# The last attention's gate: sigmoid on ScalarE, or exponential on ScalarE with an addition and a reciprocal on VectorE

## The chip, the cores and the metric

The kernel runs on one core of a Trainium2 chip. A core has a matrix engine (PE; its loading of weights is listed apart as PEld), a vector engine (DVE), an engine for activation functions (ACT), a general engine (POOL), and a queue engine that only starts transfers here (SP). The engines run their own queues of instructions in order and wait for one another through semaphores. The metric is device time in microseconds, the median of several runs.

## The reference

The reference is a decoder of four layers, each with two attentions and a feed-forward part, twelve blocks in all, on an input of 8 batches x 256 positions x 128 channels. The block that the change touches is the eleventh, `L3_xattn`: 16 heads of 8 channels, causal, with a mask over keys, and a gate on the output. `query` is the normalised input, `key` and `value` are the first 256 positions of a context:

```
q, k, v = heads(query @ Wq.T), heads(key @ Wk.T), heads(value @ Wv.T)
scores = q . k / sqrt(8), masked by key and by position
context = softmax(scores) . v, heads put side by side
gate = sigmoid(query @ Wg.T + bg)
output = (gate * context) @ Wo.T
```

The gate has 8 x 256 x 128 elements, in float32.

## The kernel before, in words

Four of the twelve blocks are attentions with 16 heads, and all four are written by one function, `_heads_attention` (L469); the last of them calls it with `causal=True`, a `key_bias` and `gate=True` (L819 to L820). Its main loop (L679) goes over steps t, one head of one batch at each: t = 16 b + h, 128 steps and a tail. What belongs to a head is spread over several steps:

- At step t `maxima` (L501) makes the scores of head t on PE into a PSUM bank (`mh_sps`), and DVE finds each row's maximum, in two instructions for the causal halves (L514, into `mh_nm`). The banks are three (`ps_a`, L487), shared with the output products.
- After every fourth head, `turn` (L535) splits the four heads' maxima on POOL (three instructions, L540 to L543, into `mh_nx`). Two steps later `turned` (L545) transposes them on PE (`mh_mps`), copies them on ACT (`mh_m`, L552), and ACT starts the transfer that puts them beside the queries (L554).
- Twelve steps behind its maxima, `exps` (L556) makes the scores of the head again, transposed, lowered by the maxima and masked, on PE (`mh_bsps`), and ACT takes the exponential (`mh_e`, L574).
- Every four heads, four steps further, `combine` (L602) multiplies the exponentials with the values on PE, sixteen products for four heads (`mh_ops`), and ACT copies the result out (L617). Two of these later `divide` (L621) transposes them back (`mh_otps`), and DVE takes the reciprocals of the sums (L631, L632) and multiplies (L636, into `mh_o`). With the batch's last heads, POOL multiplies with the gate (L643). Projection, addition to x and the norm for the next block follow (L646 to L661).
- At h = 6 of each batch, ahead of that step's maxima, `gate_of` (L594) makes the batch's gate: four products on PE (`mh_gps`), the bias added on DVE (L599), the sigmoid on ACT (L600). The gate tiles, `mh_gates`, have two buffers.

Keys and queries of the next batch are projected and spread by SP's transfers during the current batch.

The order of instructions within each engine is found by a scheduler that goes by its own estimate of when the inputs are ready; among instructions that are ready the one written earlier comes first. For the products and transposes of the attentions this is switched off: they keep the order in which they are written (L451, L454). ACT computes its functions from tables, and the instruction that loads a set of tables, `ACT_TABLE_LOAD`, isn't written in the kernel: the compiler puts it in ahead of a function where needed.

Of the kernel before, what the change touches and what calls it, by code (L numbers as in the profile page):

```python
# [35 lines left out]
AF = mybir.ActivationFunctionType  # L36
ALU = mybir.AluOpType
# [307 lines left out]
class _Heads:  # L345
# [104 lines left out]
    def mm(self, *a, **kw):  # L450
        return self.E.tc.keep_in_program_order(self.E.nc.tensor.matmul(*a, **kw))  # L451
# [17 lines left out]
def _heads_attention(E, ctx, causal=False, mask=None, key_bias=None, gate=False, guest=None, known=(0,), pace=None):  # L469
# [6 lines left out]
    hd, nc, W = E.heads, E.nc, E.w(E.heads.layer)  # L476
    n, ready = hd.n, hd.ready
    nk = n // P
    scale = DH ** -0.5
# [110 lines left out]
    outs, osbs, gates = {}, {}, {}  # L590
# [3 lines left out]
    def gate_of(b):  # L594
        ps = pg.tile([P, 2, D], F32, tag="g", name="mh_gps")
        for c in range(2):
            mm(ps[:, c, :], E.xt(b)[:, c * P : c * P + P], W("wg"), start=True, stop=True)
        gates[b] = gp.tile([P, 2, D], F32, name="mh_gates")
        nc.vector.tensor_tensor(gates[b], ps, W("bg").unsqueeze(1).to_broadcast([P, 2, D]), ALU.add)  # L599
        nc.scalar.activation(gates[b], gates[b], AF.Sigmoid)  # L600

    def combine(i):  # L602

# [75 lines left out]
    while t < end or todo:  # L679
        now[0] = t  # L680
        b, h = divmod(t, H)
# [14 lines left out]
        if gate and b < B and h == 6:  # L696
            gate_of(b)
# [1058 lines left out]
```

## Time and profile before

| | us |
|---|---|
| median of 3 runs | 1811.19 (1810.04 to 1814.04) |
| the profiled execution | 1812.43 |
| its span, first to last instruction | 1810.6 |
| first and last bias addition of a gate begin (L599) | 1559.4, 1708.0 |

Busy over the whole span:

| engine | us | share |
|---|---|---|
| PE | 1485.5 | 82% |
| PEld | 1069.0 | 59% |
| DVE | 1136.2 | 63% |
| ACT | 891.7 | 49% |
| POOL | 501.6 | 28% |

Times within the trace are counted from the start of the span. A line of the timeline gives start and duration in us, the engine, the line of the kernel, the operation, the tile written and the tiles read, shape and count; in brackets stands how long the engine was idle just before, and whose work ended that idle time. The lines of waits give the engine and tile that waited, for whom, the total in us, how often, and the longest.

### The profile page before, as it was taken

How to read it: one execution, taken by the hardware profiler on the slowest of the kernel's cores; microseconds unless marked ns; L12 is line 12 of the kernel's file. 1: busy time of each engine (PE TensorE's matmuls, PEld its weight loads, DVE VectorE, ACT ScalarE, POOL GpSimd, SP SyncE). 2: the span in 40 equal slices, each digit the busy share in tenths (PEclk: the TensorE clock that was granted, in tenths of full speed). 3: DMA queues.
4: the chain of work that ended last, by engine and by line, in shares of the span. 5: the costliest groups of instructions: out<-in, count | busy, mean ns of one | idle time of the engine just before them, and what ended most of it. 6: DMA issues, size and time to landing. Idle time of an engine off the chain costs nothing. (4 is left out here: it accounts for less than half of the span.)

```text
span 1810.6 us, 29331 instructions
## 1 busy us (share of the span) xinstructions
PE 1485.5 (82%) x10141; PEld 1069.0 (59%) x10141; DVE 1136.2 (63%) x3845; ACT 891.7 (49%) x1822; POOL 501.6 (28%) x998
## 2 busy tenths in 40 slices
PE   5689999999989989777378888879837799789976
PEld 3456677766655556354256665646516677677753
DVE  4567666665636676777377777666466555455555
ACT  7245445555642345222635556456644456466631
POOL 3122222222101121333323433331113433344331
PEclk9799999999989999897689999989967899899996
DMA  4011101114000000000111111011002321111100
GB/s 151 12 36 35 26 14 37 35 32 159 9 1 1 1 1 1 0 1 1 26 43 35 36 29 34 14 36 44 11 18 54 99 54 45 51 49 49 29 1 24
DMA packets 47236, 60.43 MB, mean 33 GB/s; under 512 B 5232, under 2 KB 36976, under 8 KB 46448
## 3 DMA queue, kind: packets, MB, share of 16 engines
q1 hardware_dynamic: 44720, 56.99, 11.9%
q8 instruction: 80, 1.31, 0.3%
q10 hardware_dynamic: 2368, 1.57, 0.3%
q14 instruction: 68, 0.56, 0.1%
HBM read 14.50 MB, written 1.05 MB: 9 GB/s over the span
## 5 line engine op out<-in xcount | busy, mean ns | idle before, releaser
L451 PE MATMUL mh_sps<-mh_k,mh_q 96*128 96x512 f32 (+2 forms) x1024 | 323.5, 398 | 48.2 <-DMA mh_q<-mh_qp 23.9
L451 PE MATMUL mh_bsps<-mh_q,mh_k 128*128 128x256 f32 (+1 forms) x1536 | 354.9, 337 | 7.0 <-ACT mh_e L587 4.1
L587 ACT ACTIVATE mh_e<-mh_bsps 128x512 f32<-128x512 f32 x512 | 280.9, 600 | 119.6 <-PE mh_bsps L451 112.4
L451 PEld LDWEIGHTS mh_bsps<-mh_q,mh_k 128*128 128x128 f32 x1536 | 267.8, 199 | 32.3 <-issue 6.7
L451 PEld LDWEIGHTS mh_sps<-mh_k,mh_q 96*128 96x128 f32 x1024 | 173.3, 203 | 94.9 <-issue 46.9
L514 DVE CUSTOM_DVE_ANT_0 mh_rest<-mh_sps,mask_b 128x512 bf16<-128x512 f32 x256 | 167.1, 684 | 80.9 <-PE mh_sps L451 77.6
L451 PE MATMUL mh_ops<-mh_e,mh_v 128*32 128x256 f32 (+1 forms) x3072 | 204.9, 380 | 11.9 <-ACT mh_e L574 10.6
L533 DVE TENSOR_REDUCE mh_nm<-mh_sps 128x1 f32<-128x512 f32 x256 | 165.0, 680 | 36.9 <-PE mh_sps L451 36.4
L451 PEld LDWEIGHTS mh_ops<-mh_e,mh_v 128*32 128x32 f32 x3072 | 97.5, 113 | 85.0 <-ACT mh_e L574 21.1
L574 ACT ACTIVATE mh_e<-mh_bsps 128x384 f32<-128x384 f32 x256 | 117.2, 493 | 53.5 <-PE mh_bsps L451 30.9
L197 POOL TENSOR_SCALAR ln_rstd<-ln_mv 128x2 f32<-128x2 f32 x96 | 22.0, 229 | 404.6 <-DVE ln_mv L195 404.2
L514 DVE CUSTOM_DVE_ANT_0 mh_rest<-mh_sps,km_q 128x128 bf16<-128x128 f32 (+1 forms) x256 | 80.0, 350 | 66.2 <-PE mh_sps L451 64.5
L540 POOL CAST mh_hi<-mh_nm 128x8 fp32r<-128x8 f32 x128 | 24.8, 194 | 338.9 <-DVE mh_nm L514 203.0
L514 DVE CUSTOM_DVE_ANT_0 mh_rest<-mh_sps,causal 128x128 bf16<-128x128 f32 (+1 forms) x256 | 79.4, 352 | 54.5 <-PE mh_sps L451 51.8
L215 ACT COPY xt<-ln_ps 128x256 f32<-128x256 f32 x96 | 36.1, 376 | 128.3 <-PE ln_ps L454 65.9
L451 PE MATMUL mh_bsps<-mask_t,ident 128*128 128x512 bf16 x256 | 98.8, 386 | 0.4 <-ACT mh_e L587 0.4
L617 ACT COPY mh_osb<-mh_ops 128x256 f32<-128x256 f32 x128 | 47.6, 372 | 89.3 <-PE mh_ops L451 89.1
L552 ACT CAST mh_m<-mh_mps 8x256 fp32r<-8x256 f32 x128 | 46.1, 360 | 91.0 <-PE mh_mps L454 89.6
L882 ACT ACTIVATE moe_si<-moe_gps 128x512 f32<-128x512 f32 x64 | 38.0, 597 | 101.9 <-PE moe_gps L880 81.1
L880 PE MATMUL moe_ups<-xt,w_L_ffn 128*128 128x512 f32 x128 | 69.6, 626 | 6.9 <-ACT moe_si L882 4.8
L201 DVE TENSOR_SCALAR ln_z<-x,ln_mv,ln_rstd 128x128 f32<-128x128 f32 x128 | 41.9, 368 | 50.5 <-POOL ln_rstd L198 50.5
L891 PEld LDWEIGHTS moe_dps<-w_L_ffn,moe_act 128*128 128x128 f32 x512 | 64.1, 199 | 15.9 <-issue 7.7
(359 smaller groups left out, 3098.3 us busy)
## 6 DMA issues: line engine op xcount, KB each, us to landing
mh_k<-mh_kp SPq DMA_DIRECT2D x64, 256.0 KB
mh_q<-mh_qp SPq DMA_DIRECT2D x256, 64.0 KB
mh_k<-mh_kp SPq DMA_DIRECT2D x64, 128.0 KB
w_L_ffn<-in_w_L_ffn SPq DMA_DIRECT2D x2, 1558.0 KB
w_L_attn<-in_w_L_attn SPq DMA_DIRECT2D x2, 1056.0 KB
ctx_t<-in_ctx_t SPq DMA_DIRECT2D x4, 512.0 KB
mh_q<-mh_m ACTq DMA_DIRECT2D x128, 8.0 KB
w_L_ffn<-in_w_L_ffn SPq DMA_DIRECT2D x2, 687.0 KB
```

The costliest lines, as they stand in the source:

```text
L201: (engine or nc.vector).tensor_scalar(z[:, q, :], E.x[:, 2 * b + q, :], mv[:, q, 0:1], rstd[:, q : q + 1], ALU.subtract, ALU.mult)
L215: E.nc.scalar.copy(E.xt(b), ps.rearrange("p q t -> p (q t)"))
L451: return self.E.tc.keep_in_program_order(self.E.nc.tensor.matmul(*a, **kw))
L514: nc.vector.tensor_tensor_reduce(rest[:, : scores.shape[1]], scores, lowered, -1.0, -FLOOR, ALU.add, ALU.min, accum_out=at)
L533: nc.vector.tensor_reduce(u.nm[:, c, col], ps, AX.X, ALU.max, negate=True)
L552: nc.scalar.copy(m, ps[:8].rearrange("p c q -> p (c q)"))
L574: nc.scalar.activation(e, ps, AF.Exp, scale=scale)
L587: nc.scalar.activation(e, ps, AF.Exp, scale=scale)
L617: nc.scalar.copy(osbs[b][:, u4 % 2, :], ops)
L880: nc.tensor.matmul(ps, W("w13")[:, o : o + P], xt, start=True, stop=True)
L882: nc.scalar.activation(si, pgate, AF.Silu)
L891: nc.tensor.matmul(ps[:, t, :], act[:, c, t * P : t * P + P], W("w2")[:, o : o + P], start=c == 0, stop=c == 1)
```

## The change

The gate's sigmoid on ACT becomes an exponential of the negated sum on ACT, an addition of 1 on DVE, and a reciprocal on DVE, all in place in the same tile: 1 / (1 + exp(-x)). Nothing else is edited.

```diff
@@ -597,7 +597,10 @@
             mm(ps[:, c, :], E.xt(b)[:, c * P : c * P + P], W("wg"), start=True, stop=True)
         gates[b] = gp.tile([P, 2, D], F32, name="mh_gates")
         nc.vector.tensor_tensor(gates[b], ps, W("bg").unsqueeze(1).to_broadcast([P, 2, D]), ALU.add)
-        nc.scalar.activation(gates[b], gates[b], AF.Sigmoid)
+
+        nc.scalar.activation(gates[b], gates[b], AF.Exp, scale=-1.0)
+        nc.vector.tensor_scalar(gates[b], gates[b], 1.0, None, ALU.add)
+        nc.vector.reciprocal(gates[b], gates[b])
 
     def combine(i):
 
```

## The prediction

> **What bounds the kernel now.** I read, in this order, the tile view of the gates, the times by stretches, the waits of PE in the last attention (1545 to 1735 us), and one gate in the timeline of each engine.
>
> The tile's and the line's view say when gates are made and what comes with them (columns: count, shortest/median/longest ns, first and last start):
>
> ```profile
> L600 ACT ACT_TABLE_LOAD  x8: 1283/1283/1283, 1560.1 to 1708.6; - x8
> L600 ACT ACTIVATE mh_gates<-mh_gates x8: 416/417/417, 1561.4 to 1709.9; 128x256 f32<-128x256 f32 x8
> L643 POOL TENSOR_TENSOR mh_o<-mh_o,mh_gates x8: 726/730/737, 1590.1 to 1734.9; 128x256 f32<-128x256 f32 x8
> ```
>
> Each of the eight sigmoids has a table load ahead of it; the groups of ACT in that stretch show eight more, of 1283 ns, ahead of the exponential that follows (L574). The gate is read some 30 us after it was begun, so its own lateness harms nobody. Next one batch, busy us of PE, PEld, DVE, ACT, POOL, then the granted clock:
>
> ```profile
> 1622.70:1644.80 22.10, 19.81 (x182) 16.04 (x181) 12.21 (x81) 14.74 (x33) 9.88 (x26) 1.00 0.19 50
> ```
>
> PE is busy for 19.8 of 22.1 us: the bound. What matters is what stops it. PE's waits (us in total, times, longest):
>
> ```profile
> PE mh_ops L451 <- ACT mh_e L574: 10.6, 7, 1.5
> PE mh_mps L454 <- POOL mh_nx L543: 4.2, 8, 1.3
> ```
>
> Seven waits of 1.5 us on ACT's exponentials, and each stands at a gate: all but the first, where no output product runs yet. The fifth gate on ACT:
>
> ```profile
> 1642.77 0.62 ACTq L554 DMA_DIRECT2D mh_q<-mh_m  x1
> 1643.43 0.49 ACT L574 ACTIVATE mh_e<-mh_bsps 128x384 f32<-128x384 f32 x1 [0.70 <-PE mh_sps L451]
> 1643.94 1.28 ACT L600 ACT_TABLE_LOAD   x1
> 1645.23 0.42 ACT L600 ACTIVATE mh_gates<-mh_gates 128x256 f32<-128x256 f32 x1
> 1645.67 1.28 ACT L574 ACT_TABLE_LOAD   x1
> 1646.96 1.25 ACT L574 ACTIVATE mh_e<-mh_bsps 128x384 f32<-128x384 f32 x3
> ```
>
> From 1643.94 to 1646.96 ACT does nothing for the attention. PE meanwhile:
>
> ```profile
> 1645.38 0.62 PE L451 MATMUL mh_ops<-mh_e,mh_v 128*32 128x256 f32 x4
> 1647.51 1.22 PE L451 MATMUL mh_ops<-mh_e,mh_v 128*32 128x256 f32 x12 [1.50 <-ACT mh_e L574]
> 1648.65 0.49 PE L451 MATMUL mh_sps<-mh_k,mh_q 96*128 96x128 f32 x2
> 1648.99 0.38 PE L454 MATMUL mh_mps<-ident,mh_nx 128*8 128x128 f32 x2
> ```
>
> The output products stop until the exponentials come; behind them, in PE's fixed order, stand the next head's scores (mh_sps) and the turning of the maxima (mh_mps), which needs DVE's maxima of the four heads before, by way of POOL. DVE there:
>
> ```profile
> 1643.88 0.42 DVE L514 CUSTOM_DVE_ANT_0 mh_rest<-mh_sps,km_q 128x256 bf16<-128x256 f32 x1
> ...
> 1644.26 0.17 DVE L631 TENSOR_SCALAR mh_rs<-mh_otps 128x16 f32<-128x16 f32 x1
> 1644.47 0.25 DVE L632 RECIPROCAL mh_rs<-mh_rs 128x16 f32<-128x16 f32 x1
> 1644.64 0.23 DVE L514 CUSTOM_DVE_ANT_0 mh_rest<-mh_sps,km_q 128x128 bf16<-128x128 f32 x1
> ...
> 1645.06 0.41 DVE L514 CUSTOM_DVE_ANT_0 mh_rest<-mh_sps,km_q 128x256 bf16<-128x256 f32 x1
> ...
> 1649.19 0.29 DVE L514 CUSTOM_DVE_ANT_0 mh_rest<-mh_sps,km_q 128x128 bf16<-128x128 f32 x1 [3.15 <-PE mh_sps L451]
> ```
>
> DVE is full until 1646 (divide, norm statistics and maxima fall together), then idle for 3.15 us, since PE stands. The change puts its DVE work into the full part.
>
> **The change, part by part.** *Removed: 16 table loads.* 8 at L600 and 8 at L574, 16 x 1.283 = 20.5 us of ACT. ACT is not the bound; the worth is in PE's stalls. Without loads the gate's exponential ends at 1643.94 + 0.42 = 1644.36, the two exponentials that the output products lack end near 1644.86 and 1645.6 (PE ends the second's scores at 1644.81; 0.2 to 0.3 of hand-over as elsewhere, then 0.5), and the sixteen products run through in 1.15 us, as between gates, from 1645.38 to 1646.53. PE could then turn the maxima at about 1646.86 (its input is there at 1646.81) in place of 1648.99: 2.13 us a gate, 14.9 us over seven. That is the gain if DVE cost nothing.
>
> The Trainium skill, "ScalarE: Activation LUTs", section "What ACT_TABLE_LOAD costs", gives 1283 ns for the load and 1380 ns more for a drain. The load agrees to the nanosecond; the drain doesn't show, since the exponential ended at 1643.92 and the load began at 1643.94. By the page the 16 switches would be 42.6 us of ACT in place of 20.5, and a gate would have held ACT over 5 us; the timeline has 3.0, and decides.
>
> *Sigmoid to exponential with scale -1.* Same shape and engine; 0.417 us is kept. Ends: nothing, and 0.08 us more (the 384-wide L574 has 0.494). It costs nothing: it stands where the sigmoid stood. No DMA is issued or moved; SP's and POOL's queues keep all theirs.
>
> *Added: addition on DVE, 128x256.* Nearest row L1267 at this width, both operands in SBUF with constants: 0.29 us.
>
> *Added: reciprocal on DVE, 128x256.* The trace has none wider than 32 columns. Its rows are 154 ns at 1 column, 199 at 8, 252 at 16, 347 at 32: 6.2 ns a column, so 148 + 256 x 6.2 = 1.74 us. Ends: 0.39 us (L599, an addition of this shape), and 8 x 0.347 = 2.78 us (eight of the 32-wide). I take 1.74, since four rows lie on that line; with the slopes 5.9 and 6.75 it would be 1.67 and 1.86.
>
> *The new wait.* The addition waits for ACT's exponential. Ready at 1644.36, it would start at about 1644.43; queued behind it on DVE are the divide (L631, L632) and, above all, the maxima of head 7, the last of their four. The order of DVE's queue is the scheduler's, oldest work first as it comes ready; the gate is older than the divide and than head 7's maxima, so I put addition and reciprocal in front of those, L631 between the two. Then reciprocal 1644.77 to 1646.51, and L632 at 1646.46 in place of 1644.47: 1.99 us later, as is all behind it. The maxima end at 1645.48 + 1.99 = 1647.47, POOL's three steps and the hand-overs take 0.73 (three rows from 1646.20 to 1646.81, with 0.07 before and 0.05 after), and PE turns the maxima at 1648.20. The next head's scores also want a bank, of three, that head 7's maxima free at 1647.5, and fit in before. So PE stops for DVE where it stopped for ACT, and the gain is 1648.99 - 1648.20 = 0.79 a gate: 5.5 us over seven. After that DVE catches up in the idle time that it had.
>
> *The first gate.* No output product waits here, so the loads cost PE nothing; DVE is behind (PE waits 0.38 us for mh_nm at 1560.45 and 0.42 for mh_nx at 1561.67), and the granted clock is low. 2 us of DVE ahead of head 7's maxima go to PE whole; if they come behind them, some 0.8 (the idle times of DVE that follow, 0.66 and 1.15 us, take up the rest). I take 1.6 of loss.
>
> Sum: 5.5 - 1.6 = 3.9 us faster. The profiled execution took 1812.43 (span 1810.6), so 1808.5; it lies 1.2 above the median of the runs, 1811.19, which goes to 1807.3. With the first gate at 0.8 or 2.0 and the reciprocal at 1.67 or 1.86, the gain is between 2.5 and 5.2.
>
> **The rivals.** *The reciprocal lands behind head 7's maxima.* The scheduler sees the exponential done a few tenths later, or holds the reciprocal for the addition, and the maxima, ready at 1644.64 to 1645.06, slip in. For it: the two must both be issued in 0.7 us. Against: the gate is older. Then the stall goes, but for up to 0.6 a gate for head 8's bank: 7 x (1.5 to 2.1) - 0.8, 10 to 14 us faster, 1797 to 1801.
>
> *The addition stands at the head of DVE's queue.* Placed straight behind L599 (done at 1643.75), it holds DVE for 0.7 us until ACT is done. The gain of a gate falls to 0.1 and the first costs 2.6: 2 slower, 1813. Against: between L599 and 1644.36 head 6's maxima were ready.
>
> *The reciprocal is dearer than its line* (the other side). A gate gains 0.79 less what it takes beyond 1.74; with the first gate the sum is zero at 1.74 + 3.9 / 8 = 2.2 us, and slower by 0.2% (3.6 us) from 2.7. At 2.78: 8 x 1.04 - 3.9 = 4.4 slower, 1815.6. For it: from 32 to 256 columns nothing is shown. Against: the four rows.
>
> *Eight cycles a column.* In this kernel that would be a reciprocal between the line and its upper end, with the stall kept about as long as today: the time before, 1811 to 1812. The Trainium skill, "VectorE: DVE Perf Modes", section "Walkthrough: the 8-slice pipeline in each mode", has the reciprocal iterate with a repeat count of 8, which at its 0.96 GHz is an estimated 8.3 ns a column, 2.1 us and some; the rows of the trace say 6.2.
>
> *The change doesn't do what it says*, a load staying ahead of L600 or L574: every other function of the stretch ran without one between gates. Left out.
>
> **How the numbers follow.** 0.2%, 3.6 us, is about what a measurement of this kernel can tell from no change. Forecast 0.50, with its centre at 3.9, so split as 0.30 faster and 0.20 same; reciprocal behind the maxima 0.22, faster; addition in front 0.08 and eight cycles 0.05, same; dear reciprocal 0.15, slower. Together 0.52, 0.33, 0.15. Likeliest 1807.3, its own range 1806 to 1809. The range of 8 in 10 takes in most of the faster rival and the small losses: 1798 to 1814.
>
> **What would show it.** In the profile after: no load at L600 or L574 in the last attention; the waits of mh_ops on mh_e gone; PE at each gate waiting instead for mh_nm or mh_nx, near 1.3 us; the reciprocal near 1.74 us, ahead of head 7's maxima; DVE's idle 3.15 us shorter; a batch of 21.3 us in place of 22.1. Wrong if the wait on mh_nx is absent (then 10 or more faster), if the reciprocal is over 2.2 us, or if DVE idles before the addition.

## The result, and the profile after

The changed kernel is faster: ratio 0.9961 to the kernel before, with a 95% interval of 0.9947 to 0.9975 (medians 1806.76 and 1811.81 us, 13 runs each). On 1811.8 us that is 7.1 us, between 4.5 and 9.6; the two medians lie 5.1 us apart. The forecast was 3.9 us, with a range of its own of 2.5 to 5.2: right in direction and in the main of its mechanism, too small in size by the ratio.

The profiled execution after took 1797.04 us, 15.4 less than that of before, and not all of this is the change. Up to the last attention the two kernels have the same instructions in the same order on every engine, yet the first gate begins at 1551.9 us in place of 1559.4. The changed kernel's own runs lie between 1797 and 1811. So what follows compares the last attention alone, from gate to gate.

First the gates, in the tile view of the kernel after (columns as before; lines below the change are numbered three higher):

```profile
L601 ACT ACTIVATE mh_gates<-mh_gates x8: 407/408/416, 1552.6 to 1695.9; 128x256 f32<-128x256 f32 x8
L602 DVE TENSOR_SCALAR mh_gates<-mh_gates x8: 287/289/291, 1553.6 to 1696.9; 128x256 f32<-128x256 f32 x8
L603 DVE RECIPROCAL mh_gates<-mh_gates x8: 1740/1743/1748, 1554.1 to 1697.2; 128x256 f32<-128x256 f32 x8
```

No table load is left at the gate, and none at L574 in this attention. The addition takes 0.289 us and the reciprocal 1.743. PE's waits in the stage (1530 to 1725 us):

```profile
PE mh_mps L454 <- POOL mh_nx L543: 9.7, 15, 1.4
...
PE mh_sps L451 <- ACT mh_osb L620: 3.4, 7, 0.5
...
PE mh_sps L451 <- DVE mh_nm L514: 1.2, 2, 0.8
```

The seven waits on mh_e, 10.6 us, are gone. In their place stand seven more waits for the split maxima (9.7 us in all where there were 4.2) and seven of 0.5 us for a bank. The fifth gate on DVE:

```profile
1633.74 0.39 DVE L599 TENSOR_TENSOR mh_gates<-mh_gps,w_L_xattn 128x256 f32<-128x256 f32 x1
...
1635.02 0.23 DVE L514 CUSTOM_DVE_ANT_0 mh_rest<-mh_sps,km_q 128x128 bf16<-128x128 f32 x1
...
1635.17 0.29 DVE L602 TENSOR_SCALAR mh_gates<-mh_gates 128x256 f32<-128x256 f32 x1
1635.37 0.22 DVE L639 TENSOR_TENSOR mh_o<-mh_otps,mh_rs 128x64 f32<-128x64 f32 x1
1635.51 1.74 DVE L603 RECIPROCAL mh_gates<-mh_gates 128x256 f32<-128x256 f32 x1
...
1637.24 0.41 DVE L514 CUSTOM_DVE_ANT_0 mh_rest<-mh_sps,km_q 128x256 bf16<-128x256 f32 x1
```

The reciprocal lies between the two halves of head 7's maxima. In the kernel before, the bias addition of this gate is

```profile
1643.36 0.39 DVE L599 TENSOR_TENSOR mh_gates<-mh_gps,w_L_xattn 128x256 f32<-128x256 f32 x1
```

The second half ran 1.70 us after the bias addition began in the kernel before (1645.06 after 1643.36), and now 3.50 us after it: 1.80 us late. PE at the same gate:

```profile
1635.76 0.86 PE L451 MATMUL mh_ops<-mh_e,mh_v 128*32 128x256 f32 x16
1637.11 0.49 PE L451 MATMUL mh_sps<-mh_k,mh_q 96*128 96x128 f32 x2 [0.49 <-ACT mh_osb L620]
1638.39 0.38 PE L454 MATMUL mh_mps<-ident,mh_nx 128*8 128x128 f32 x2 [0.79 <-POOL mh_nx L543]
```

The sixteen output products now run in one piece, and PE then stands for the bank and for the maxima. From the bias addition to mh_mps it was 5.63 us before (1643.36 to 1648.99) and is 4.65 now: 0.98 us gained.

The starts of the bias addition (L599), in each kernel's timeline of DVE, give the distance of the gates:

| us from gate to gate | 1-2 | 2-3 | 3-4 | 4-5 | 5-6 | 6-7 | 7-8 |
|---|---|---|---|---|---|---|---|
| before | 17.70 | 21.99 | 22.11 | 22.14 | 22.10 | 22.12 | 20.43 |
| after | 18.57 | 21.00 | 21.13 | 21.15 | 21.13 | 21.15 | 19.45 |

Six distances are each 0.97 to 0.99 shorter, 5.9 us together; the first, with the first gate, is 0.87 longer. The last gate gains 0.98 as well (mh_mps 5.63 us after the bias addition before, 4.65 after). So the attention itself gives 6.0 us, inside the measured 4.5 to 9.6.

### The profile page after: what moved, and what is told of

It reads as the page before. It is cut to its first block, busy times and chain, and to the rows that moved or that the text cites. A ratio compares the mean times of both kernels' runs of the same rounds, so it can differ in the third digit from the quotient of the medians.

```text
span 1795.3 us, 29269 instructions
## 1 busy us (share of the span) xinstructions
PE 1476.0 (82%) x10103; PEld 1067.2 (59%) x10141; DVE 1149.9 (64%) x3861; ACT 871.3 (49%) x1806; POOL 502.6 (28%) x998
## 5 line engine op out<-in xcount | busy, mean ns | idle before, releaser
L451 PE MATMUL mh_sps<-mh_k,mh_q 96*128 96x512 f32 (+2 forms) x1024 | 323.7, 398 | 54.2 <-DMA mh_q<-mh_qp 24.1
L451 PE MATMUL mh_ops<-mh_e,mh_v 128*32 128x256 f32 (+1 forms) x3072 | 193.7, 373 | 1.3 <-DVE mh_nm L514 0.8
L574 ACT ACTIVATE mh_e<-mh_bsps 128x384 f32<-128x384 f32 x256 | 118.7, 493 | 59.5 <-PE mh_bsps L451 36.2
L451 PE MATMUL mh_bsps<-mask_t,ident 128*128 128x512 bf16 x219 | 85.0, 388 | 0.4 <-ACT mh_e L587 0.4
L454 PE MATMUL mh_mps<-ident,mh_nx 128*8 128x128 f32 x256 | 50.9, 281 | 28.8 <-POOL mh_nx L543 24.2
```

The costliest lines, as they stand in the source:

```text
L454: return self.E.tc.keep_in_program_order(self.E.nc.tensor.transpose(*a))
L574: nc.scalar.activation(e, ps, AF.Exp, scale=scale)
```

## The experiments

Three readings were to be told apart. A, that of the prediction: the loads' removal is worth 2.1 us a gate, and DVE's new work, in front of head 7's maxima, takes half of it back. B: in the changed kernel it is the bank freed by ACT's copy that holds PE. C: the gain was made elsewhere. All ratios are to the kernel before, with 95% intervals; distances are those of the middle gates, 3 to 7. The diffs are against the changed kernel where nothing else is said.

| kernel | ratio | gate to gate |
|---|---|---|
| before | 1 | 22.1 |
| after | 0.9961 (0.9947 to 0.9975) | 21.1 |
| exp_only | 0.9927 (0.9904 to 0.9951) | 20.0 |
| late | 0.9927 (0.9910 to 0.9944) | 20.0 |
| tanh | 0.9934 (0.9912 to 0.9956) | 20.1 |
| sigmoid_and_dve | 0.9995 (0.9981 to 1.0010) | 22.1 |
| late_twice | 0.9988 (0.9972 to 1.0003) | 21.2 |
| recip_one_and_half | 1.0065 (1.0044 to 1.0086) | 22.0 or 23.3 |
| recip_twice | 1.0094 (1.0072 to 1.0116) | 24.1 |

**exp_only: the loads alone.**

```diff
         nc.scalar.activation(gates[b], gates[b], AF.Exp, scale=-1.0)
-        nc.vector.tensor_scalar(gates[b], gates[b], 1.0, None, ALU.add)
-        nc.vector.reciprocal(gates[b], gates[b])
```

> The exponential stays on ACT; the addition and the reciprocal on DVE are left out, so the gate is exp(-x) and not the sigmoid. This shows what the 16 table loads are worth by themselves. Theory A (a gate's gain of 2.1 us is half taken back by DVE work that lies in front of the maxima of head 7): gates 20.0 us apart where they were 22.1 before and are 21.1 after the change; PE waits at the gates neither for mh_e nor for mh_nx beyond 0.1 us; 14 to 15 us faster than the kernel before. Rival B (in the changed kernel PE is held at each gate by the bank that ACT's copy mh_osb frees, and DVE's lateness lies beside that): gates 20.6 us apart or more, 8 to 11 us faster. Rival C (the gain was made ahead of the first gate, where the two profiles already lie 7.5 us apart, and not at the gates): gates 21 us apart, 5 to 7 us faster.

Gates 20.0 us apart, as A expected, and not as B and C did. Sixteen loads are worth 2.1 us a gate. PE waits for mh_e at no gate. For the split maxima, the waits in the stage are now

```profile
PE mh_mps L454 <- POOL mh_nx L543: 5.7, 14, 1.7
```

At the third gate and all that follow, PE waits 0.18 to 0.20 us for them, where A allowed 0.1. At the fifth gate it turns them 3.51 us after the bias addition began; in the kernel before this was 5.63. The whole, 13.2 us, is a little under what A gave, and the first distance shows why: it grew from 17.70 to 21.70 us. PE comes to the second batch's first scores 8.42 us after the first gate (8.79 in the kernel before), but it begins them at 11.34, where the kernel before began at 8.97. It stands in between for something the profile doesn't name (the transfers that spread that batch's queries are under way then). PE's timeline, and then two stretches of the stage (length, busy us of PE, PEld, DVE, ACT, POOL, granted clock, DMA share, GB/s):

```profile
1571.29 0.77 PE L451 MATMUL mh_sps<-mh_k,mh_q 96*128 96x128 f32 x2 [2.92 <-issue]
```

```profile
1570.00:1574.00 4.00, 2.71 (x21) 1.78 (x21) 0.64 (x4) 0.49 (x1) 0.25 (x1) 0.53 0.13 33
1574.00:1578.00 4.00, 4.00 (x21) 3.39 (x18) 1.29 (x8) 2.02 (x5) 0.40 (x1) 0.61 0.01 2
```

The clock is 0.53 and 0.61 there; in the kernel before it was 1.00 at the same distance from the first gate.

**late: the same work at another place in DVE's queue.**

```diff
-        nc.vector.tensor_scalar(gates[b], gates[b], 1.0, None, ALU.add)
-        nc.vector.reciprocal(gates[b], gates[b])
+        def invert():
+            nc.vector.tensor_scalar(gates[b], gates[b], 1.0, None, ALU.add)
+            nc.vector.reciprocal(gates[b], gates[b])
+
+        later(2, invert)
```

> The same three instructions, but the addition and the reciprocal are written two steps later, behind the maxima of head 8, so that DVE's queue has them where DVE stood idle for 3.15 us before the change. Theory A: the work is the same and costs nothing there: reciprocal 1.74 us, gates 20.0 to 20.2 us apart, 13 to 14 us faster than the kernel before (the first gate may lose up to 0.9). Rival B: 20.6 apart or more, 8 to 11 faster. Rival C: as the changed kernel, 5 to 7 faster.

As A expected: 20.0 us apart and 13 us faster, with the reciprocal about as long as in the changed kernel (1.753 us). Only the first distance is longer than was allowed: 2.45 us more than in the kernel before (20.15), where up to 0.9 was expected. At the fifth gate, DVE and then PE:

```profile
1637.17 0.39 DVE L599 TENSOR_TENSOR mh_gates<-mh_gps,w_L_xattn 128x256 f32<-128x256 f32 x1
...
1639.76 0.44 DVE L604 TENSOR_SCALAR mh_gates<-mh_gates 128x256 f32<-128x256 f32 x1
1640.24 1.75 DVE L605 RECIPROCAL mh_gates<-mh_gates 128x256 f32<-128x256 f32 x1
```

```profile
1639.18 0.86 PE L451 MATMUL mh_ops<-mh_e,mh_v 128*32 128x256 f32 x16
1639.97 0.49 PE L451 MATMUL mh_sps<-mh_k,mh_q 96*128 96x128 f32 x2
1640.72 0.38 PE L454 MATMUL mh_mps<-ident,mh_nx 128*8 128x128 f32 x2 [0.25 <-POOL mh_nx L543]
```

The reciprocal now stands behind the maxima of head 8 and runs until 1641.99. It keeps head 9's maxima waiting until 1641.91, but PE doesn't need their bank before the scores of head 12, at 1642.74. So mh_mps stands 3.55 us after the bias addition, nearly as without DVE's work (3.51). B falls with this too: the wait for ACT's copy is gone as soon as DVE is on time. It went along with DVE's lateness and was no cause of its own. This kernel computes the same as the changed one and is faster than both: its interval ends where that of the changed kernel hasn't begun.

**tanh: another function, one instruction on DVE.**

```diff
-        nc.scalar.activation(gates[b], gates[b], AF.Exp, scale=-1.0)
-        nc.vector.tensor_scalar(gates[b], gates[b], 1.0, None, ALU.add)
-        nc.vector.reciprocal(gates[b], gates[b])
+        nc.scalar.activation(gates[b], gates[b], AF.Tanh, scale=0.5)
+        nc.vector.tensor_scalar(gates[b], gates[b], 0.5, 0.5, ALU.mult, ALU.add)
```

> The gate as 0.5 + 0.5 tanh(x/2): tanh on ACT and one DVE instruction with two constants, no reciprocal; the gate's value is the same. Theory A with tanh in the set of tables that holds the exponential: no load in the last attention, 0.2 to 0.3 us of DVE in front of head 7's maxima, gates 20.2 us apart, 13 to 14 us faster than the kernel before. If tanh needs another set: 16 loads as before, gates 22.1 apart, 0 to 2 us slower than before. Rival B: 20.6 apart or more, 8 to 11 faster.

No load is left in the attention, and the tanh takes 0.408 us like the exponential. The gates are 20.1 apart, 0.1 more than without any DVE work: the instruction's 0.29 us lie between the two halves of head 7's maxima, and only a part shows. The whole is 12.0 us, a little under the 13 to 14 expected; the first distance grew here too, to 21.94 us, with a wait of 2.48 us that the profile doesn't name. The Trainium skill, "ScalarE: Activation LUTs", section "Table sets: the hidden batching unit", puts exp and tanh into one set and sigmoid into another; the traces agree, with 16 loads for the sigmoid and none for tanh.

**recip_twice: the suspected cost doubled in its place.**

```diff
         nc.vector.reciprocal(gates[b], gates[b])
+        nc.vector.reciprocal(gates[b], gates[b])
```

> The changed kernel with the reciprocal made twice, so that the gate is 1 + exp(-x) and not the sigmoid; it doubles the suspected cost where it lies. Theory A: each gate is 1.66 us longer (a reciprocal less its overlap with the next instruction), gates 22.8 us apart, the wait of mh_mps on mh_nx 2.4 us in place of 0.8; 13 us slower than the changed kernel, 6 to 8 us slower than the kernel before. Rivals B and C: DVE is not what PE waits for, gates stay within 0.5 us of 21.1, 3 to 7 us faster than before.

DVE is what PE waits for, but by more than A said: 24.06 us from gate to gate, 2.93 more than after, where 1.66 was expected, and 17 us slower than before, where 6 to 8 were expected. The wait is as expected; the rest is the clock behind it:

```profile
1655.08 0.38 PE L454 MATMUL mh_mps<-ident,mh_nx 128*8 128x128 f32 x2 [2.46 <-POOL mh_nx L543]
...
1657.90 0.73 PE L451 MATMUL mh_sps<-mh_k,mh_q 96*128 96x128 f32 x2
```

```profile
1652.00:1656.00 4.00, 1.42 (x11) 1.15 (x11) 3.46 (x13) 0.44 (x2) 0.55 (x3) 1.00 0.14 36
1656.00:1660.00 4.00, 4.00 (x32) 3.37 (x31) 1.93 (x12) 2.12 (x5) 2.02 (x5) 0.57 0.10 25
```

In the 4 us from 1656 on, behind the wait, the granted clock is 0.57 in the mean, and the scores take 0.73 us where they take 0.44 to 0.49 at full clock.

**recip_one_and_half: a wait between the two.**

```diff
         nc.vector.reciprocal(gates[b], gates[b])
+        nc.vector.reciprocal(gates[b][:, 0, :], gates[b][:, 0, :])
```

> The changed kernel with a second reciprocal of half the gate, 128 columns, right behind the first (half of the gate's values are then 1 + exp(-x) and not the sigmoid). With the reciprocal made twice the gates were 24.06 us apart where 22.8 was expected; the rest lay in a low clock, 0.57, after PE's 2.5 us of waiting. Theory A with a threshold between 0.8 and 2.5 us of waiting: the wait of mh_mps grows by 0.87 us to 1.65, the clock stays at 1.00, gates 22.0 us apart, 6 to 8 us slower than the changed kernel, within 2 us of the kernel before. If any longer wait lowers the clock: gates 22.6 us or more, 4 us or more slower than the kernel before.

The wait is 1.65 us as expected, and the kernel is slower than theory A had it: 11.8 us slower than before (8.0 to 15.6), where 2 at most were expected. The distances explain it: 24.62, 21.98, 23.25, 23.28, 21.98 and 21.58 us from the second gate on. Where the clock stays, it is the 22.0 that A gives; at other gates the same wait ends with a low clock and costs some 1.3 us more, and over 2.6 us more at the second gate, where the low clock lasts longest. The fifth gate is one of these:

```profile
1654.50:1658.50 4.00, 1.95 (x15) 1.68 (x16) 3.34 (x16) 0.71 (x2) 0.58 (x4) 1.00 0.17 45
1658.50:1662.50 4.00, 4.00 (x31) 2.90 (x30) 1.51 (x10) 2.29 (x6) 2.01 (x5) 0.57 0.15 39
```

So neither of the two expectations holds as put. In the middle batches, the clock never fell behind the changed kernel's two waits (0.49 and 0.79 us) and always fell behind those of recip_twice (0.49 and 2.46); with 0.49 and 1.65 it falls at some gates and not at others, so at this length the wait alone doesn't decide.

**sigmoid_and_dve: the loads and DVE's work together.**

```diff
         nc.scalar.activation(gates[b], gates[b], AF.Sigmoid)
+        nc.vector.tensor_scalar(gates[b], gates[b], 1.0, None, ALU.add)
+        nc.vector.reciprocal(gates[b], gates[b])
```

(The diff is against the kernel before.)

> The sigmoid with its table loads stays, and addition and reciprocal on DVE are made as well, in place (the gate is then 1 / (1 + sigmoid) and not the sigmoid). In the order of DVE's queue they lie behind the maxima of head 8, where DVE stands idle for 3.15 us in the kernel before. Theory A (it is the place in DVE's queue that costs, not DVE's time): PE waits for mh_e 1.5 us at each gate as in the kernel before, the DVE work is hidden, gates 22.1 to 22.3 us apart, from no change to 2 us slower than the kernel before. Rival (1.9 us of DVE a gate cost wherever they lie): gates 24 us apart, 13 us slower.

No difference from the kernel before, and the old wait is there again:

```profile
PE mh_ops L451 <- ACT mh_e L574: 10.6, 7, 1.5
```

Two microseconds of DVE cost nothing here, since they lie where DVE has nothing to do: the reciprocal ends 1.00 us before the next maxima can start, those of head 9:

```profile
1654.29 0.29 DVE L514 CUSTOM_DVE_ANT_0 mh_rest<-mh_sps,km_q 128x128 bf16<-128x128 f32 x1 [1.00 <-PE mh_sps L451]
```

**late_twice: how much fits behind.**

```diff
         def invert():
             nc.vector.tensor_scalar(gates[b], gates[b], 1.0, None, ALU.add)
             nc.vector.reciprocal(gates[b], gates[b])
+            nc.vector.reciprocal(gates[b], gates[b])
```

(The diff is against late.)

> The late form with the reciprocal made twice (the gate is then 1 + exp(-x) and not the sigmoid): as much DVE work as the doubled reciprocal that cost 2.9 us a gate, but behind head 8's maxima; a pair of maxima comes between the two. Theory A: 20.0 to 20.5 us between gates, no clock below 1.00 after the second gate, 11 to 14 us faster than the kernel before. Rival (DVE's time costs wherever it lies): 21.7 us or more between gates, 2 us faster or less.

The miss lies between the two readings: 21.2 us from gate to gate, 1.2 more than with one reciprocal, and no sure gain over the kernel before. DVE and PE at the fifth gate:

```profile
1647.90 0.23 DVE L514 CUSTOM_DVE_ANT_0 mh_rest<-mh_sps,km_q 128x128 bf16<-128x128 f32 x1
...
1648.05 1.75 DVE L606 RECIPROCAL mh_gates<-mh_gates 128x256 f32<-128x256 f32 x1
1649.71 0.36 DVE L514 CUSTOM_DVE_ANT_0 mh_rest<-mh_sps,km_q 128x256 bf16<-128x256 f32 x1
```

```profile
1650.14 0.50 PE L451 MATMUL mh_sps<-mh_k,mh_q 96*128 96x128 f32 x2 [1.25 <-DVE mh_nm L514]
```

The second reciprocal fell between the halves of head 9's maxima and held their bank; three heads on, PE wanted it for the scores of head 12. The clock was at 1.00 from the second gate on, as expected. So DVE's work is not free at the later place, it has room there for one reciprocal. In front of head 7, the same two reciprocals cost 4.1 us a gate, the clock's part included (24.06 less 20.0); here 1.2.

## Why the prediction was right, and by how much it was off

- *The loads.* 16 went, and a gate without DVE work gained 2.1 us (22.1 to 20.0), as worked out (2.13).
- *The reciprocal's price.* 1.74 us was taken from four narrow rows, and 1.743 was measured. (The upper slope, 6.75, comes from rows of 253 ns at 16 columns; with the 252 that the prediction gives it is 6.6, and the range stays.) The rivals of a dearer reciprocal and of eight cycles a column (a little over 2.1 us) fall with this.
- *The exponential and the addition.* 0.417 kept, 0.408 found; 0.29 taken, 0.289 found.
- *Place in the queue.* Forecast in front of head 7's maxima, with L631 between addition and reciprocal; found between the two halves of those maxima, with a multiplication between. For PE it is the same, since the split maxima need the second half. But the order by age that the forecast rests on did not come out: the divide (L634, L635) and the first half, both younger than the gate, went ahead of the addition, and why is not shown. Behind the second half it would have been the rival that puts the work behind head 7, so it is in part luck that the price came out nearly as forecast. That rival and the one that lets the addition stand first did not occur; late shows what the first one is worth, 13 us against the 10 to 14 that were worked out.
- *What is late next.* The wait on mh_nx, 0.79 us, took the place of the wait on mh_e, as forecast. That the scores of head 9 would wait for ACT's copy, 0.49, was not foreseen; it costs nothing of its own, since without it PE would only have waited longer for the split maxima. Together the two waits are 1.28 us, near the 1.3 that were forecast.
- *The term that was off: the gain of a gate,* 0.79 forecast, 0.98 measured. Of delay 1.99 us were forecast and 1.80 measured. 0.17 of the forecast was the addition waiting for the exponential, but the exponential was done at 1634.61, half a microsecond before DVE came to the addition. Over seven gates that is 1.3 us.
- *The first gate,* 1.6 us of loss forecast, 0.87 longer distance found. PE's new wait there is 0.82 us for the maxima's bank, near the lower case of 0.8 that the prediction named. Two more things differ: in stretches of 2 us, the granted clock of the kernel before is back at 1.00 from 8 us after the first gate on, that of the changed one from 12 us on; and the kernel before stands 0.94 us within this distance for something the profile doesn't name, which the changed one doesn't. How the 0.87 is made up of these stays open: this first distance lies between 17.7 and 21.9 us over the nine profiles, with a clock between 0.5 and 1.0, and sigmoid_and_dve has 19.92 with no change in PE's waits at the other gates.

With these two terms as measured, the forecast 3.9 becomes 6.0. What the measured ratio holds beyond the 6.0, about one microsecond, is within its interval and isn't claimed.

## What to carry to other kernels

A stall that an engine's table loads cause is worth taking away, but its worth is read from what stands next in the waiting engine's order: here half the possible gain went to work that the change itself had put in front of the maxima PE needed next. When work moves to another engine, ask where in that engine's queue it lands and who needs the instruction behind it; the same reciprocal cost 1.1 us a gate in one place and next to nothing two steps later (21.1 and 20.0 us from gate to gate, 20.0 without it). And where one function can be had through another whose table is already loaded (tanh for the sigmoid), most of the move isn't needed: one DVE instruction of 0.29 us was left of it.

## What the runs showed of the hardware that was not expected

A wait of PE costs more than its length when the clock falls behind it. Waits of 1.50 us (before) and of 0.49 and 0.79 (after) left the granted clock at 1.00 in the middle batches. Waits of 0.49 and 1.65 (recip_one_and_half) lowered it, to 0.57 over 4 us at the fifth gate, at some gates and not at others, and cost some 1.3 us more each time in the middle batches. Waits of 0.49 and 2.46 (recip_twice) lowered it at every gate from the second on, and made the middle distances 1.27 us longer than the wait explains; 2.92 us in exp_only went with clocks of 0.53 and 0.61. The Trainium skill, "TensorE: Matmul & The Clock Gate", section "HAM oscillation — how this bites in real kernels", gives as its rule no idle gap of PE over some 3.4 us; these gaps are shorter, and the measurement decides. The same page of the Trainium skill, section "What's actually happening", says that the activity is judged over a window that runs freely; that would fit equal waits with unequal clocks, but no run here shows the window.

A float32 reciprocal on DVE goes by its width: 154 ns at 1 column, 347 at 32, 953 at 128 (recip_one_and_half) and 1743 at 256, which is 6.2 ns a column from end to end.
